# One more step ahead of six uses in the layer norm and feed-forward, and another way to lay out weights in the head, of a one-core scan kernel

## The chip, the cores and the metric

The kernel runs on one core of a Trainium2 chip. The metric is the device time of one launch in microseconds (us). The core has five engines with instruction streams of their own: TensorE (PE, with its weight loads shown as PEld), VectorE (DVE), ScalarE (ACT), GpSimd (POOL) and SyncE (SP), which here only issues DMAs.

## What is computed

The input is x, 4 images of 64x64 pixels with 96 channels. One launch runs a convolution and scan block, an attention block and a feed-forward block. The reference, cut to its main lines:

```python
def selective_scan(u, delta, A, Bs, Cs, D, delta_bias):
    delta = softplus(delta + delta_bias[None, :, :, None])
    def step(h, inp):
        ut, dt, Bt, Ct = inp
        dA = exp(dt[..., None] * A[None])
        h = dA * h + (dt * ut)[..., None] * Bt[:, :, None, :]
        return h, einsum('bkdn,bkn->bkd', h, Ct)
...
xp, z = split(bilinear(x, W_in, s_in, b_in), 2, axis=-1)      # sign weights, sign inputs
t = conv3x3(sign(xp + move0_b), Wb); t = prelu(t + conv_b + rp_b0) + rp_b1 + xp
xs = four directions of silu(t)                               # rows, columns, both reversed
dts, Bs, Cs = split(bilinear(xs, Wl, sl, bl)); dts = bilinear(dts, Wd, sd, bd)
A = -exp(A_logs)
y = sum of the four selective_scan outputs, each turned back to row order
y = (y - mean(y)) / sqrt(var(y) + 1e-5) * ln_w + ln_b
out = bilinear(y * silu(z), W_out, s_out, b_out)
```

192 channels with 16 states each are scanned over 4096 positions in 4 directions for each of the 4 images. The attention and feed-forward blocks that follow have layer norms of their own, over 96 channels.

## The kernel before, in words

**The order is written out by hand.** Instructions go to each engine's stream in the order in which the Python code issues them, and every engine is in order. Generators (`yield`) interleave the parts: a step is what a generator issues between two yields.

**The pieces.** `Scans.run` walks 1536 pieces, 384 an image, 96 a direction; the directions go in the order 1, 3, 0, 2. A piece is 32 of the channels with 4 of the states (128 partitions) by 1024 positions. For each piece ScalarE computes the decay `dA` (an Exp into PSUM, two buffers, L1531); GpSimd the injection `w` = dl times bc (L443, three pieces ahead); VectorE the scan (L443); VectorE or GpSimd the product with C (L443), chosen by `Tally`, which adds up estimated time for either; and TensorE the sum over states (L1604, four pieces later). L443 is the helper that counts, so many instructions share that line.

**The background.** After every piece `run` takes one step of one generator, `back`: the rest of image 0's prologue (projection, convolution, projections for the scan), the prologue of image 1, and then for each image: the turn of its fourth direction, the prologue of the image two further on, the layer norm and attention sums (`Epilogue.sums`, which calls `norm` for 8 blocks q of 512 columns, 11 steps each), the turn of the next image if its scans are far enough, and the feed-forward (`Epilogue.last`, 8 blocks of 12 steps). In `norm` and `last` a step typically writes a product into PSUM and the next step uses it: yc (L1131) by the square sq (L1191), the variance var by its logarithm (L1200), xc by xq (L1247), xv by `rstd` (L1136), kv (L1259) by kvs (L1264), and in `last` fv by `rstd`. The last image's norm and feed-forward run partly after the scans, in four lanes.

**The turn.** `turn` (L985 to L1013) loads the second column direction's output in 16 parts (yt, five of them ahead), copies each transposed into yh on ScalarE (L1003), and stores yh in two halves of 1.5 MB; yh has one buffer. `run` needs the turn of an image from its fourth direction on:

```python
            if i % NQ == 1:
                while KORD[self.pieces[i][1]] == 2 and self.pieces[i][0] not in c.turned:
                    next(back)
```

These lines (L1718) run the background on until the turn is done, ahead of piece i's other work.

**The head.** `weights` (from L160) loads and signs the weights while image 0's prologue starts; two steps of the prologue go to each one of `weights`. GpSimd's `omad` (L289) comes from the scales of the convolution (L276 to L289, reductions on VectorE); `transposed` (L193 to L201) puts transposes into one of two PSUM banks (y0, y1, shared with the prologue's projections ix and iz) and casts them out on VectorE. Delta's weights wd are transposed once (two calls), and 8 and 16 small stores (L331, L336) lay them on the diagonals of wdz and wdy. A's logs come in one load (al, L400), go through Exp on ScalarE (L402) and a sign change on VectorE (L403), and six DMAs (L405) lay them out as anm. The convolution's weighted row sums use a product with a ones matrix (tpw, L359). The prologue of image 0 runs 16 parts (2 halves by 8 blocks of 512 columns): ix and iz (L647, L648), tp (L653), the convolution cv (L745), v (L783), r (L784), the gate, u (L443), and copies for the next step.

**The DMA queue.** All loads and stores but a few small ones go through SP, in order; `Later` issues a store two steps after it was asked for (L462).

Of the kernel before, what the change touches and what calls it, by code (L numbers as in the profile page):

```python
# [53 lines left out]
def hybrid_kernel(ctx: ExitStack, tc: tile.TileContext, a: dict, out: bass.AP):  # L54
# [108 lines left out]
    def weights():  # L163
# [72 lines left out]
        nc.sync.dma_start(wo, a["w_out"])  # L236
        small = {}
# [18 lines left out]
        for t in gTs + [wdz, wdy]:  # L256
            nc.gpsimd.memset(t.bitcast(F32), 0.0)
# [16 lines left out]
        part = temp("part", [96, 2, 2])  # L274
        for i in range(2):
            for h in range(2):  # L276
                nc.vector.tensor_reduce(part[:, h, i : i + 1], cwn[h][i], AX.X, ALU.add, apply_absolute_value=True)
            yield
        nc.vector.tensor_tensor(csc, part[:, :, 0], part[:, :, 1], ALU.add)
        nc.vector.tensor_scalar(csc, csc, 1.0 / (9 * DN), None, ALU.mult)  # L280

        nc.vector.tensor_tensor(cbias, pv[:, :, CONV_B], pv[:, :, RP0], ALU.add)
        nc.vector.tensor_tensor(acs, pv[:, :, PRELU], csc, ALU.mult)
        nc.vector.tensor_tensor(acb, pv[:, :, PRELU], cbias, ALU.mult)
        nc.vector.tensor_tensor(acb, acb, pv[:, :, B_X], ALU.add)
        nc.vector.tensor_tensor(acb, acb, pv[:, :, RP1], ALU.add)
        nc.vector.tensor_scalar(oma, pv[:, :, PRELU], -1.0, 1.0, ALU.mult, ALU.add)
        for h in range(2):
            nc.gpsimd.tensor_scalar(omad[:, h], i96, oma[:, h : h + 1], None, ALU.mult)  # L289
        yield  # L290
# [5 lines left out]
        for o in range(2):  # L296
            m = negmean(f"wlm{o}", wl[o], DN)
            sw = temp(f"wls{o}", [128, DN], BF16)
            nc.scalar.activation(sw, wl[o], AF.Sign, bias=m)
            we = temp(f"wle{o}", [128, 4, 128], BF16)  # L300
            nc.gpsimd.memset(we, 0.0)
            for kk in range(2):
                rows = slice(64 * kk, 64 * kk + 64)
                for x, pair in enumerate(kinds[kk]):
                    for half, j in enumerate(pair):
                        if j is not None:
                            to, src = we[rows, x, 64 * half : 64 * half + 64], sw[rows, 64 * j : 64 * j + 64]
                            if o:
                                to = we[rows, x, half::2]
                            else:  # L310
                                to, src = to.rearrange("p (e i) -> p i e", e=2), src.rearrange("p (i e) -> p i e", e=2)
                            nc.gpsimd.tensor_copy(to, src)
            yield
            yield
            transposed(wR[:, o].rearrange("p x m -> p (x m)"), [we[:, x, :] for x in range(4)])
            yield


        wdt = []
        for x, t in enumerate(wd):  # L320
            wdm = negmean(f"wdm{x}", t, NR)
            wds = temp(f"wds{x}", [128, NK, NR], BF16)
            for k in range(NK):
                nc.scalar.activation(wds[:, k, :], t[:, k, :], AF.Sign, bias=wdm[:, k : k + 1])
            wdt.append(temp(f"wdt{x}", [NR, NK * 32]))
            yield
            transposed(wdt[x].bitcast(F8), [wds[:, k, :] for k in range(NK)])
            yield
        one, two = (t.rearrange("c (k d) -> c k d", k=NK) for t in wdt)
        for s in range(8):  # L330
            nc.sync.dma_start(wdz.bitcast(F32)[NR * s : NR * s + NR, :, s, :], one)  # L331
        yield
        for r0 in (0, 64):
            for s in range(8):
                at = r0 + NR * s
                nc.sync.dma_start(wdy.bitcast(F32)[at : at + NR, :, s, r0 // 4 : r0 // 4 + 16], two[:, :, 0:16])  # L336
        yield
# [12 lines left out]

        ones, diag = temp("ones", [96, 128]), temp("diag", [96, 4, 96])
        nc.vector.memset(ones, 1.0)
        for i in range(2):
            for h in range(2):
                col = pv[:, h, (LN_W, LN_B)[i] : (LN_W, LN_B)[i] + 1]
                nc.gpsimd.tensor_scalar(diag[:, 2 * i + h], i96, col, None, ALU.mult)
        yield
        ps = p.ps.tile([128, 512], F32, name="tpw", tag="y1")
        nc.tensor.matmul(ps[:, 0:384], ones, diag.rearrange("p i m -> p (i m)"), start=True, stop=True)  # L359
        for h in range(2):  # L360
            for o in range(2):
                nc.vector.tensor_tensor(
                    meanw[0:96, h, o], mean[:, int(h != o)], ps[0:96, 96 * o : 96 * o + 96], ALU.mult
                )
        nc.vector.tensor_copy(
            meanw[96:97, 0].rearrange("p o m -> p (o m)"), ps[96:97, 192:384]
        )
        yield
# [29 lines left out]
        yield  # L398
        al, al2 = temp("al", [128, 2, NK * NS]), temp("al2", [128, 2, 4, NK * NQ])
        nc.sync.dma_start(al, a["al"].rearrange("p h k s -> p h (k s)"))  # L400
        yield
        nc.scalar.activation(al, al, AF.Exp)  # L402
        nc.vector.tensor_scalar(al2, al.rearrange("p h (s j) -> p h j s", j=4), -1.0, None, ALU.mult)  # L403
        for g in range(NG):
            nc.sync.dma_start(anm[:, g, :], al2[32 * (g % 4) : 32 * (g % 4) + 32, g // 4])  # L405
# [133 lines left out]
def prologue(c, b, xts=None):  # L539
# [11 lines left out]
    with tc.tile_pool(name=f"xg_{b}", bufs=1) as xgp:  # L551
# [3 lines left out]
        with tc.tile_pool(name=f"cv_{b}", bufs=1) as cvp:  # L555
# [6 lines left out]
            def clear():  # L562
                nc.gpsimd.memset(xgw[64:128, 1], 0.0)
                for h in range(2):
                    nc.gpsimd.memset(tflat[h].bitcast(F32), 0.0)

            if alone:
                clear()

# [36 lines left out]
            def xfin(q, ps):  # L606
                n = CH if alone else 512
                cols = slice(n * q, n * q + n)
                nc.scalar.activation(xsT[:, cols], ps, AF.Sign, bias=negm, saturate=False)
                if alone:  # L610
                    t = c.p.w.tile([128, CH], F32, name=f"xb{q}_{b}", tag="w")[0:96]
                    nc.vector.tensor_scalar(t, ps, c.bo, None, ALU.add)
                else:
                    t = f32(f"xb{q}")[0:96]
# [3 lines left out]
            for q in range(4 if alone else NQ8):  # L618
                if alone:
                    ps = c.p.dA.tile([128, CH], F32, name=f"xps{q}_{b}", tag="dA")[0:96]  # L620
                    for i in range(8):
                        nc.tensor.transpose(ps[:, 128 * i : 128 * i + 128], xts[q][:, i, :], ident)
                else:
                    ps = bank(f"xps{q}", q % 2)[0:96]
                    for i in range(4):
                        nc.tensor.transpose(ps[:, 128 * i : 128 * i + 128], xts[q // 2][:, 4 * (q % 2) + i, :], ident)
                yield
                xfin(q, ps)
# [4 lines left out]
            if not alone:  # L633
                clear()
# [99 lines left out]
            def alone_parts():  # L734

                mid = end = None
                for n, part in enumerate(parts + [None, None]):
# [4 lines left out]
                    for s in range(4):  # L742
# [271 lines left out]
class Epilogue:  # L1014
# [143 lines left out]

    def norm(self, ln, q, got):
# [28 lines left out]
        yield  # L1188
        for h in range(2):
            t = f32(f"sq{h}")  # L1190
            nc.scalar.activation(t, sq[h], AF.Square)  # L1191
            sq[h] = t
# [5 lines left out]
        yield  # L1198
        sd, var, eps = (f32("sd"), ps[0:96], c.eps5[0:96]) if alone else (y0[96:97], ps[96:97], c.eps5[96:97])
# [45 lines left out]
        yield  # L1245
        t = f32("xq")
# [3 lines left out]
        yield  # L1250
        r = self.rstd(ln, f"xr{q}", ps)
# [8 lines left out]
        yield  # L1260
        kv = []
# [27 lines left out]
    def last(self, ln):  # L1289
# [25 lines left out]
        while nxt:  # L1315
# [28 lines left out]
            yield  # L1344
            r = self.rstd(ln, f"fr{q}", ps)
# [43 lines left out]
class Scans:  # L1389
# [250 lines left out]
    def start(self):  # L1640
# [35 lines left out]
        while lanes:  # L1676
            interleave(lanes)
        for n in range(3):
# [135 lines left out]
```

## Time and profile before

| | |
|---|---|
| median of 9 runs | 5379.89 us (5369.27 to 5382.63) |
| the profiled execution | 5372.74 us, of which the span is 5370.7 |
| granted TensorE clock, mean | 0.738 |
| first scan, last scan start | 184.26 us, 5248.73 us |
| busy: VectorE, GpSimd, ScalarE, TensorE | 93%, 92%, 67%, 63% |
| one scan (128x1024), one injection, one decay | 2.34, 2.36, 1.12 us |
| one product with C on VectorE, on GpSimd | 1.23, 2.36 us |

The profile shows one execution. Its page has the busy time of each engine, the span in 40 slices with the busy share of each in tenths, and groups of instructions of one line. A line of the waits reads: engine, the tile it was about to work on, what it waited for, then the total in us, how many times, and the longest. A line of the timeline reads: start, duration, engine, line, operation, tiles, count, and in brackets the idle time ahead of it with what ended it. In the windows view a line is one stretch: start and end, its length, then the busy time of PE, PEld, DVE, ACT and POOL with their instruction counts, the granted clock, the DMA share and GB/s.

### The profile page before, as it was taken

The numbers are of one execution on the slowest core, as the hardware profiler recorded it, in microseconds if no ns is written. First come the engines' busy times: TensorE is split into PE (matmuls) and PEld (weight loads), VectorE is DVE, ScalarE is ACT, GpSimd is POOL, SyncE is SP. The second block draws the span as 40 slices with busy tenths as digits, with TensorE's granted clock in tenths as the row PEclk, the third lists the DMA queues.
The fourth block names the chain that finished last, engine by engine and source line by source line (L and its number), as shares of the span: only waits on it lengthen the run. The fifth ranks groups of instructions, "written<-read, shape, count | busy, mean of one in ns | idle before, by whom it ended". The sixth has DMA issues, their size and how long they took to land. (4 is left out here: it accounts for less than half of the span.)

```text
span 5370.7 us, 61933 instructions
## 1 busy us (share of the span) xinstructions
PE 3377.4 (63%) x20029; PEld 1341.8 (25%) x20029; DVE 5005.1 (93%) x3163; ACT 3614.0 (67%) x5644; POOL 4954.6 (92%) x2255
## 2 busy tenths in 40 slices
PE   7357765467645776656775587566776664444577
PEld 3212222122222332212222233122232221111223
DVE  5699999999999999998999999999999999999995
ACT  6577767687766667777777666677656775565554
POOL 4699999999999999998999999999999999999990
PEclk8667877678866886777886678677787666666788
DMA  5666666867765666676765666766666565665652
GB/s 108 177 199 197 210 186 204 256 202 216 223 192 179 216 202 203 201 235 212 216 212 178 206 216 196 246 202 208 205 214 197 177 206 195 195 221 197 216 176 65
DMA packets 605500, 1068.83 MB, mean 199 GB/s; under 512 B 219740, under 2 KB 336885, under 8 KB 603381
## 3 DMA queue, kind: packets, MB, share of 16 engines
q1 hardware_dynamic: 602788, 1063.93, 64.1%
q8 instruction: 157, 2.57, 0.2%
q14 instruction: 171, 1.39, 0.1%
q0 software_dynamic: 1536, 0.79, 0.1%
q10 hardware_dynamic: 848, 0.15, 0.0%
HBM read 829.69 MB, written 228.30 MB: 197 GB/s over the span
## 5 line engine op out<-in xcount | busy, mean ns | idle before, releaser
L443 POOL TENSOR_TENSOR w<-dl,bc 128x1024 f32<-128x1024 f32 x1524 | 3551.1, 2357 | 54.4 <-PE yp L1604 31.3
L1531 ACT ACTIVATE dA<-dl,anm 128x1024 f32<-128x1024 f32 x1524 | 1701.2, 1116 | 488.9 <-DVE w L443 299.2
L443 DVE TENSOR_TENSOR_SCAN dA<-dA,cy,w 128x1024 f32<-128x1024 f32 x725 | 1698.5, 2343 | 75.9 <-ACT dA L1531 61.8
L443 POOL TENSOR_TENSOR w<-h,bc 128x1024 f32<-128x1024 f32 x570 | 1342.2, 2355 | 113.3 <-DVE h L443 106.9
L1604 PE MATMUL yp<-w,sum 128*32 128x256 f32 x12288 | 1246.6, 502 | 296.8 <-ACT pd L1485 208.8
L443 DVE TENSOR_TENSOR w<-dA,bc 128x1024 f32<-128x1024 f32 x966 | 1183.2, 1225 | 73.9 <-DMA bc<-bcd 11.0
L443 DVE TENSOR_TENSOR_SCAN h<-dA,cy,w 128x1024 f32<-128x1024 f32 x427 | 999.2, 2340 | 5.2 <-ACT dA L1531 4.6
L1604 PEld LDWEIGHTS yp<-w,sum 128*32 128x32 f32 x12288 | 317.0, 127 | 1352.7 <-issue 746.9
L1573 ACT COPY cy<-dA 128x1 f32<-128x1 f32 x725 | 113.9, 157 | 760.9 <-DVE w L443 758.3
L443 DVE TENSOR_TENSOR_SCAN dA<-dA,w 128x1024 f32<-128x1024 f32 x241 | 550.0, 2282 | 27.1 <-ACT dA L1531 24.2
L1466 PE MATMUL dps<-gT,wdz 128*128 128x64 fp8e5 x1008 | 114.5, 313 | 376.3 <-ACT ys L1618 374.4
L443 DVE TENSOR_TENSOR_SCAN h<-dA,w 128x1024 f32<-128x1024 f32 x143 | 325.9, 2279 | 22.4 <-POOL w L443 10.2
L1479 PE MATMUL dps<-sp,ident 128*128 128x512 f32 x378 | 263.4, 785 | 103.3 <-ACT dps L1475 103.2
L1609 PE MATMUL yp<-ya,back 128*128 128x256 f32 x576 | 219.9, 500 | 0.0
L1466 PEld LDWEIGHTS <-wdz 128*128 128x128 fp8e5 x1008 | 94.0, 152 | 452.0 <-issue 451.8
L1466 PE MATMUL dps<-gT,wdy 128*128 128x64 fp8e5 x504 | 57.6, 314 | 207.3 <-ACT ys L1618 207.2
L806 PE MATMUL cv<-tp,cwA 128*96 128x512 fp8e5 x432 | 150.9, 467 | 37.6 <-ACT r L838 36.5
L1573 ACT COPY cy<-h 128x1 f32<-128x1 f32 x427 | 79.2, 185 | 133.1 <-DVE h L443 132.4
L1131 PE MATMUL yc<-eys,mean 96*96 96x512 f32 x240 | 137.3, 726 | 48.2 <-DVE vks L443 24.4
L1471 ACT ACTIVATE pd<-dps,dbias,pvd 128x512 f32<-128x512 f32 x189 | 143.8, 761 | 9.0 <-PE dps L1466 8.9
L1472 ACT ACTIVATE sp<-dps,dbias,pvd 128x512 f32<-128x512 f32 x189 | 144.8, 766 | 0.0
L1609 PEld LDWEIGHTS yp<-ya,back 128*128 128x128 f32 x576 | 115.2, 231 | 117.3 <-issue 89.1
(379 smaller groups left out, 4488.1 us busy)
## 6 DMA issues: line engine op xcount, KB each, us to landing
dl<-dld SPq DMA_DIRECT2D x762, 512.0 KB
bc<-bcd SPq DMA_DIRECT2D x512, 512.0 KB
dld<-pd SPq DMA_DIRECT2D x126, 512.0 KB
yd<-ys SPq DMA_DIRECT2D x764, 64.0 KB
dld<-pd SPq DMA_DIRECT2D x126, 256.0 KB
ya<-yd SPq DMA_DIRECT2D x192, 128.0 KB
pu<-ud SPq DMA_DIRECT2D x32, 512.0 KB
pu<-utd SPq DMA_DIRECT2D x31, 512.0 KB
```

Source lines behind the costliest of these rows:

```text
L443: return getattr(self.eng, name)(out, *args, **kw)
L806: nc.tensor.matmul(ps, w[:, 96 * h : 96 * h + 96], tp[:, 8 * q + dy : 8 * q + dy + 8, dx : dx + IW], start=(w is taps[0][1]), stop=(w is t ...
L1131: self.c.nc.tensor.matmul(ps, w, x, start=(i == 0), stop=(i == len(pairs) - 1))
L1466: nc.tensor.matmul(pv[:, s], wd[:, k, s], gT[:, :, c0 : c0 + 16], start=(s == 0), stop=(s == 7))
L1471: nc.scalar.activation(d[:, 0], ps, AF.Abs, scale=sc, bias=bi)
L1472: nc.scalar.activation(t, ps, AF.Relu, scale=sc, bias=bi)
L1479: nc.tensor.matmul(ps, c.ident, t, start=False, stop=True, skip_group_check=True)
L1531: c.nc.scalar.activation(t, self.dlt[i // NQ][0], AF.Exp, scale=c.anm[:, g, NQ * KORD[e] + q : NQ * KORD[e] + q + 1])
L1573: self.c.nc.scalar.copy(self.carries[g, q], h[:, CH - 1 : CH])
L1604: c.nc.tensor.matmul(y[32 * x : 32 * x + 32, g % 2, :], c.sum4, prod[:, 256 * x : 256 * x + 256], start=(q == 0), stop=(q == NQ - 1 and no ...
L1609: c.nc.tensor.matmul(y[:, g % 2, :], w, src, start=False, stop=(n == len(more) - 1))
```

## The change

There are two parts. **In the epilogue** `room` adds one more yield, so one more piece, between six products and their first use, for images 0, 1 and 2: five in `norm` (ahead of sq, var's logarithm, xq, the rstd of xv, kvs) and one in `last` (the rstd of fv). **In the head** delta's signed weights are copied onto diagonals by GpSimd (40 small copies and three clears in e and wdf) and transposed in eight calls of `transposed`, eight transposes each, in place of two calls and 24 stores; the scales (and omad behind them) are computed after the first half of wR; the layer norm's weight rows come as six DMAs in place of the product with ones; A's logs come as 24 DMAs of single elements straight into anm, with Exp and sign change just before the first scan; GpSimd's clearing of xg and tp stands after the input's transposes in place of ahead of them; those are done in eight blocks of 512 columns in place of four of 1024; and u has a buffer per part and is stored in 16 parts in place of 8.

```diff
--- before.py
+++ after.py
@@ weights
+        wrow = temp("wrow", [96, 2, 96], F32)
+        for rows, h, s in halves(a["pv"][:, :, LN_W]):
+            nc.sync.dma_start(wrow[:, h, rows], s.partition_broadcast(96))
+        for rows, h, s in halves(a["pv"][:, :, LN_B]):
+            nc.sync.dma_start(meanw[96:97, 0, h, rows], s.unsqueeze(0))
...
-        for t in gTs + [wdz, wdy]:
+        for t in gTs + [wdz]:
             nc.gpsimd.memset(t.bitcast(F32), 0.0)
...
+        def scales():
+            part = temp("part", [96, 2, 2])
...
             for h in range(2):
-                nc.gpsimd.tensor_scalar(omad[:, h], i96, oma[:, h : h + 1], None, ALU.mult)
-        yield
+                nc.gpsimd.tensor_scalar(omad[:, h], i96, oma[:, h : h + 1], None, ALU.mult)
...
             transposed(wR[:, o].rearrange("p x m -> p (x m)"), [we[:, x, :] for x in range(4)])
             yield
+            if o == 0:
+                scales()
+                yield
...
-            wdt.append(temp(f"wdt{x}", [NR, NK * 32]))
-            yield
-            transposed(wdt[x].bitcast(F8), [wds[:, k, :] for k in range(NK)])
-            yield
-        one, two = (t.rearrange("c (k d) -> c k d", k=NK) for t in wdt)
         for s in range(8):
-            nc.sync.dma_start(wdz.bitcast(F32)[NR * s : NR * s + NR, :, s, :], one)
-        yield
-        for r0 in (0, 64):
-            for s in range(8):
-                at = r0 + NR * s
-                nc.sync.dma_start(wdy.bitcast(F32)[at : at + NR, :, s, r0 // 4 : r0 // 4 + 16], two[:, :, 0:16])
-        yield
+            nc.gpsimd.tensor_copy(e[:, :, s, NR * s : NR * s + NR], wds[0])
+        yield
+        for k in range(NK):
+            transposed(wdz[0:48, k].rearrange("p s d -> p (s d)"), [e[:, k, s, :] for s in range(8)])
+            yield
+        for k2 in range(0, NK, 2):
+            e = temp(f"wdf{k2}", [128, 2, 8, 128], BF16)
+            nc.gpsimd.memset(e, 0.0)
+            for r0 in (0, 64):
+                for s in range(8):
+                    at = r0 + NR * s
+                    nc.gpsimd.tensor_copy(e[r0 : r0 + 64, :, s, at : at + NR], wds[1][r0 : r0 + 64, k2 : k2 + 2])
+            yield
+            for k in range(2):
+                transposed(wdy[:, k2 + k].rearrange("p s d -> p (s d)"), [e[:, k, s, :] for s in range(8)])
+                yield
...
-                nc.gpsimd.tensor_scalar(diag[:, 2 * i + h], i96, col, None, ALU.mult)
-        yield
-        ps = p.ps.tile([128, 512], F32, name="tpw", tag="y1")
-        nc.tensor.matmul(ps[:, 0:384], ones, diag.rearrange("p i m -> p (i m)"), start=True, stop=True)
...
+                nc.vector.tensor_tensor(meanw[0:96, h, o], mean[:, int(h != o)], wrow[:, o], ALU.mult)
...
-        nc.sync.dma_start(al, a["al"].rearrange("p h k s -> p h (k s)"))
-        yield
-        nc.scalar.activation(al, al, AF.Exp)
-        nc.vector.tensor_scalar(al2, al.rearrange("p h (s j) -> p h j s", j=4), -1.0, None, ALU.mult)
         for g in range(NG):
-            nc.sync.dma_start(anm[:, g, :], al2[32 * (g % 4) : 32 * (g % 4) + 32, g // 4])
+            src = a["al"][32 * (g % 4) : 32 * (g % 4) + 32, g // 4].rearrange("d k (q j) -> j d (k q)", j=4)
+            for j in range(4):
+                nc.sync.dma_start(anm[j::4, g, :], src[j])
@@ prologue
-            if alone:
-                clear()
...
-                n = CH if alone else 512
-                cols = slice(n * q, n * q + n)
+                cols = slice(512 * q, 512 * q + 512)
...
             sub.close()
-            if not alone:
-                clear()
+            nc.gpsimd.memset(xgw[64:128, 1], 0.0)
+            for h in range(2):
+                nc.gpsimd.memset(tflat[h].bitcast(F32), 0.0)
...
-                            if eh == 0:
-                                us = c.p.h.tile([128, CH], F32, name=f"u{eq}_{b}", tag="h")[0:96]
-                            u = us[:, 512 * eh : 512 * eh + 512]
+                            u = f32("u" + en)[0:96]
                             c.vec.tensor_tensor(u, epz, e, ALU.mult)
-                            if eh:
-                                dst = c.ud[b].rearrange("h p l -> p h l")[:, :, 512 * eq : 512 * eq + 512]
-                                c.later.store(dst, us.rearrange("p (h l) -> p h l", h=2))
+                            c.later.store(c.ud[b][eh][:, 512 * eq : 512 * eq + 512], u)
@@ Epilogue
+    def room(self):
+
+        if self.b < NB - 1:
+            yield
+
...
                 sq.append(ps)
         yield
+        yield from self.room()
...
                 nc.vector.tensor_scalar(yc[h], yc[h], c.pv[:, h, LN_W : LN_W + 1], None, ALU.mult)
         yield
+        yield from self.room()
...
         mm(pc, [(c.mean96, x1)])
         yield
+        yield from self.room()
...
         mm(ps, [(c.on96, t)])
         yield
+        yield from self.room()
...
             nc.tensor.matmul(pk[i // 2][:, i % 2], tt[:, 128 * i : 128 * i + 128], c.wkv, start=True, stop=True)
         yield
+        yield from self.room()
...
             mm(ps, [(c.on96, t)])
             yield
+            yield from self.room()
             r = self.rstd(ln, f"fr{q}", ps)
@@ Scans.start
             interleave(lanes)
+        nc.scalar.activation(c.anm, c.anm, AF.Exp)
+        nc.vector.tensor_scalar(c.anm, c.anm, -1.0, None, ALU.mult)
```

More of the change, by code (lines that the diff above doesn't have):

```diff
@@ L272, in weights @@
         yield
-        part = temp("part", [96, 2, 2])
-        for i in range(2):
-            for h in range(2):
-                nc.vector.tensor_reduce(part[:, h, i : i + 1], cwn[h][i], AX.X, ALU.add, apply_absolute_value=True)
-            yield
[L279 to L289, printed above, removed]
-        yield
+        def scales():
+            part = temp("part", [96, 2, 2])
+            for i in range(2):
+                for h in range(2):
+                    nc.vector.tensor_reduce(part[:, h, i : i + 1], cwn[h][i], AX.X, ALU.add, apply_absolute_value=True)
+            nc.vector.tensor_tensor(csc, part[:, :, 0], part[:, :, 1], ALU.add)
+            nc.vector.tensor_scalar(csc, csc, 1.0 / (9 * DN), None, ALU.mult)
+            nc.vector.tensor_tensor(cbias, pv[:, :, CONV_B], pv[:, :, RP0], ALU.add)
+            nc.vector.tensor_tensor(acs, pv[:, :, PRELU], csc, ALU.mult)
+            nc.vector.tensor_tensor(acb, pv[:, :, PRELU], cbias, ALU.mult)
+            nc.vector.tensor_tensor(acb, acb, pv[:, :, B_X], ALU.add)
+            nc.vector.tensor_tensor(acb, acb, pv[:, :, RP1], ALU.add)
+            nc.vector.tensor_scalar(oma, pv[:, :, PRELU], -1.0, 1.0, ALU.mult, ALU.add)
+            for h in range(2):
+                nc.gpsimd.tensor_scalar(omad[:, h], i96, oma[:, h : h + 1], None, ALU.mult)
         kinds = (((0, 1), (2, None), (None, 0), (1, 2)), ((1, 0), (None, 2), (0, None), (2, 1)))
@@ L313, in weights @@
             yield
-            yield
             transposed(wR[:, o].rearrange("p x m -> p (x m)"), [we[:, x, :] for x in range(4)])
             yield
-        wdt = []
+            if o == 0:
+                scales()
+                yield
+        wds = []
         for x, t in enumerate(wd):
             wdm = negmean(f"wdm{x}", t, NR)
-            wds = temp(f"wds{x}", [128, NK, NR], BF16)
+            wds.append(temp(f"wds{x}", [128, NK, NR], BF16))
             for k in range(NK):
-                nc.scalar.activation(wds[:, k, :], t[:, k, :], AF.Sign, bias=wdm[:, k : k + 1])
-            wdt.append(temp(f"wdt{x}", [NR, NK * 32]))
-            yield
-            transposed(wdt[x].bitcast(F8), [wds[:, k, :] for k in range(NK)])
-            yield
-        one, two = (t.rearrange("c (k d) -> c k d", k=NK) for t in wdt)
-        for s in range(8):
-            nc.sync.dma_start(wdz.bitcast(F32)[NR * s : NR * s + NR, :, s, :], one)
-        yield
-        for r0 in (0, 64):
-            for s in range(8):
-                at = r0 + NR * s
-                nc.sync.dma_start(wdy.bitcast(F32)[at : at + NR, :, s, r0 // 4 : r0 // 4 + 16], two[:, :, 0:16])
-        yield
+                nc.scalar.activation(wds[x][:, k, :], t[:, k, :], AF.Sign, bias=wdm[:, k : k + 1])
+        e = temp("wde", [128, NK, 8, 48], BF16)
+        nc.gpsimd.memset(e, 0.0)
[4 more added lines that the diff above has]
+            transposed(wdz[0:48, k].rearrange("p s d -> p (s d)"), [e[:, k, s, :] for s in range(8)])
+            yield
+        for k2 in range(0, NK, 2):
+            e = temp(f"wdf{k2}", [128, 2, 8, 128], BF16)
+            nc.gpsimd.memset(e, 0.0)
+            for r0 in (0, 64):
+                for s in range(8):
+                    at = r0 + NR * s
+                    nc.gpsimd.tensor_copy(e[r0 : r0 + 64, :, s, at : at + NR], wds[1][r0 : r0 + 64, k2 : k2 + 2])
+            yield
+            for k in range(2):
+                transposed(wdy[:, k2 + k].rearrange("p s d -> p (s d)"), [e[:, k, s, :] for s in range(8)])
+                yield
         nc.vector.tensor_tensor(dbias, pvd[:, :, NK : 2 * NK], pvd[:, :, 2 * NK :], ALU.add)
@@ L349, in weights @@
         nc.vector.memset(mean[:, 1], -1.0 / DN)
[L351 to L355, printed above, removed]
-                nc.gpsimd.tensor_scalar(diag[:, 2 * i + h], i96, col, None, ALU.mult)
-        yield
-        ps = p.ps.tile([128, 512], F32, name="tpw", tag="y1")
-        nc.tensor.matmul(ps[:, 0:384], ones, diag.rearrange("p i m -> p (i m)"), start=True, stop=True)
         for h in range(2):
             for o in range(2):
[L362 to L367, printed above, removed]
-        yield
+                nc.vector.tensor_tensor(meanw[0:96, h, o], mean[:, int(h != o)], wrow[:, o], ALU.mult)
         nc.vector.tensor_copy(
@@ L397, in weights @@
             nc.sync.dma_start(sbR[r0 + 32 : r0 + 32 + NR, o, :], a["sl_dt"][k])
-        yield
-        al, al2 = temp("al", [128, 2, NK * NS]), temp("al2", [128, 2, 4, NK * NQ])
-        nc.sync.dma_start(al, a["al"].rearrange("p h k s -> p h (k s)"))
-        yield
-        nc.scalar.activation(al, al, AF.Exp)
-        nc.vector.tensor_scalar(al2, al.rearrange("p h (s j) -> p h j s", j=4), -1.0, None, ALU.mult)
         for g in range(NG):
-            nc.sync.dma_start(anm[:, g, :], al2[32 * (g % 4) : 32 * (g % 4) + 32, g // 4])
+            src = a["al"][32 * (g % 4) : 32 * (g % 4) + 32, g // 4].rearrange("d k (q j) -> j d (k q)", j=4)
+            for j in range(4):
+                nc.sync.dma_start(anm[j::4, g, :], src[j])
     c = SimpleNamespace(**locals())
@@ L560, in prologue @@
             sub = ExitStack()
[L562 to L565, printed above, removed]
-            if alone:
-                clear()
             if xts is None:
@@ L606, in xfin @@
             def xfin(q, ps):
-                n = CH if alone else 512
-                cols = slice(n * q, n * q + n)
+                cols = slice(512 * q, 512 * q + 512)
                 nc.scalar.activation(xsT[:, cols], ps, AF.Sign, bias=negm, saturate=False)
+                t = f32(f"xb{q}")[0:96]
                 if alone:
-                    t = c.p.w.tile([128, CH], F32, name=f"xb{q}_{b}", tag="w")[0:96]
                     nc.vector.tensor_scalar(t, ps, c.bo, None, ALU.add)
                 else:
-                    t = f32(f"xb{q}")[0:96]
                     nc.scalar.activation(t, ps, AF.Identity, bias=c.bo)
                 c.later.store(c.xbd[b][:, cols], t)
[L618 to L626, printed above, removed]
+            for q in range(NQ8):
+                ps = bank(f"xps{q}", q % 2)[0:96]
+                for i in range(4):
+                    nc.tensor.transpose(ps[:, 128 * i : 128 * i + 128], xts[q // 2][:, 4 * (q % 2) + i, :], ident)
                 yield
@@ L632, in prologue @@
             sub.close()
-            if not alone:
-                clear()
+            nc.gpsimd.memset(xgw[64:128, 1], 0.0)
+            for h in range(2):
+                nc.gpsimd.memset(tflat[h].bitcast(F32), 0.0)
             szs = {}
```

## The prediction

> **What bounds the kernel now.** I read the page's totals first.
>
> ```profile
> span 5370.7 us, 61933 instructions
> PE 3377.4 (63%) x20029; PEld 1341.8 (25%) x20029; DVE 5005.1 (93%) x3163; ACT 3614.0 (67%) x5644; POOL 4954.6 (92%) x2255
> DVE  5699999999999999998999999999999999999995
> POOL 4699999999999999998999999999999999999990
> ```
>
> VectorE and GpSimd share the work of the scan pieces (injection, scan, product) and are both full from the third slice to the last; ScalarE and TensorE have room. So a microsecond goes only if both of these two lose it: in the head (the first scan starts at 184.26), in idle time, or in work. Then I took busy time by stage: image 0's layer norm (89 pieces) and a stretch with no background work (67 pieces). The columns are the window, its length, then PE, PEld, DVE, ACT and POOL busy.
>
> ```profile
> 1712.70:2015.60 302.90, 236.09 (x1219) 90.10 (x1217) 291.30 (x193) 197.31 (x318) 293.19 (x128) 0.83 0.63 204
> 4461.50:4673.60 212.10, 87.37 (x637) 33.28 (x636) 209.13 (x120) 109.18 (x159) 208.00 (x90) 0.64 0.61 197
> ```
>
> A piece costs 302.90/89 = 3.404 us in the norm and 212.10/67 = 3.166 bare. VectorE idles 0.130 against 0.044 a piece, GpSimd 0.109 against 0.059. Third, the waits from 230 to 5280: what ScalarE waited for, and below it what VectorE and GpSimd did.
>
> ```profile
> ACT sq L1191 <- PE yc L1131: 64.8, 49, 2.9
> ACT xq L1247 <- PE xc L1131: 28.3, 24, 2.0
> ACT xr L1136 <- PE xv L1131: 25.0, 21, 2.7
> ACT kvs L1264 <- PE kv L1259: 24.6, 41, 1.2
> ACT eys L1200 <- PE var L1131: 19.6, 21, 1.8
> ACT fr L1136 <- PE fv L1131: 9.6, 10, 1.9
> ```
>
> ```profile
> DVE dA L443 <- ACT dA L1531: 86.0, 74, 2.2
> ```
>
> These are the six products of the change: a background step writes the product, one piece later ScalarE is already waiting for it, and the decay of the next piece stands behind that wait. They sum to 172 us, but VectorE waits only 86 us for decays in all: most of a 1 to 3 us wait is absorbed by the decay that is ready ahead.
>
> **The change part by part.**
>
> *1. One more step (room).* Ahead of five uses in the norm and one in the feed-forward, for images 0 to 2: 3x8x5 + 3x8x1 = 144 steps that issue nothing. A step with nothing in it costs a bare piece that would have come later anyway (stretches 1290-1357 and 1380-1470 have an idle lane), so 0 by itself. The gain is the idle time that goes. Excess idle of VectorE over bare: image 0 (0.130-0.044)x89 = 7.7; image 1 (0.137-0.044)x89 = 8.3; image 2 (0.188-0.044)x95 = 13.7: 29.6 us. Sorted by the 11 steps of a 512-column block, 0.98 us stands in the step ahead of sq and var and 0.26 in that of kv: about 1.1 above bare, x24 = 26. GpSimd's excess by the same sum: 4.5 + 5.5 + 11 = 21. Both must lose it, so 21 is the most likely ceiling; some products will still be late at one piece more, as the longest wait (2.9 us) is near a whole piece; so I take **-18**. Bounds: 0 (the idle moves to the next wait) and -44 (the norm's whole excess, 0.238x89 + 0.253x89 + 0.279x95 = 70, less its own vector work of 24x3.0 us spread over two engines = 36, is 34; and fv's 10).
>
> *2. What the longer norms push (forced turn).* The steps move the background by 40 pieces a norm and 8 a feed-forward. Image 2's turn (16 copies yh of 1.08 us each on ScalarE, with 16 loads and two 1.5 MB stores) stood at pieces 975-994; after norm 0, feed-forward 0 and norm 1 it is 80 to 88 later. Image 2's fourth direction begins at piece 1056, and L1718 then runs the background on until the turn is done: in the issue order of the changed program 13 of the 16 copies stand ahead of one decay (piece 1058). yh has one buffer, so half of them also wait for the first store to land. Price: 13x1.08 = 14; the store lands 7.7 to 11.6 us after its issue in the trace's three earlier turns, 9; the loads, only five of which are ahead, about 3: 26 us before a decay that takes 1.1. VectorE then holds two pieces, 2x3.25 = 6.5. Stall 26 + 1.1 - 6.5 = **+21**. Bounds: 14 + 1.1 - 6.5 = 9 (stores and loads hidden) and 14 + 12 + 12 + 1.1 - 6.5 = 33. Today's turn 2 costs nothing (3.141 us a piece, ScalarE idle 0.96 a piece), the cover that is lost. Image 1's turn now falls between norm 0 and feed-forward 0 and image 3's at 1407-1426 is 14 pieces before its need: neither is forced, 0.
>
> *3. The head.* Here I read the waits of 20 to 185 and the timeline. Scans start 49.4 us after xa, the last step of the convolution's prologue, and this part isn't touched; so the head's cost is the shift of the 16 convolution parts, whose v (L783) comes at 35.78, 40.85, 48.15, 57.58, 61.49, 71.23, 80.14, 92.85, 96.33 ... 127.25: 3.5 to 3.9 apart where nothing disturbs.
>
> ```profile
> POOL omad L289 <- DVE oma L287: 20.9, 1, 20.9
> ```
> ```profile
> 85.32 0.43 SPq L395 DMA_DIRECT2D sbR<-in_sl_bc  x1
> ...
> 92.32 0.31 ACT L402 ACTIVATE slab<-slab 128x128 f32<-128x128 f32 x1 [6.16 <-DMA slab<-in_al]
> ...
> 92.96 3.88 SPq L405 DMA_DIRECT2D anm<-slab  x6
> ...
> 96.47 0.59 PE L786 MATMUL cz<-xsT,winT 96*96 96x512 fp8e5 x1 [7.99 <-DVE u L443]
> ```
>
> (a) GpSimd is in order. The clearing of tp now stands behind omad, which waits for VectorE, and behind the second twelve weight copies (2.3 us), which wait for a sign on ScalarE at about 36; they end near 38.5, and the first tp can be written at about 40.4 in place of 24.46: +16. (b) Eight transposed calls of eight transposes, each with a VectorE cast of 48 or 128 x 1024 (about 1.3 us from the 0.68 of 512 columns), and GpSimd's memset and copies (4.2 us a half) take the place of two such calls. They share the y banks with the first parts; today's four such stalls of TensorE are 2.1 to 3.1 us each. At 1.4 a call: +11, so part 3 comes at 57.58 + 27 = 84.5. (c) Parts 4 to 15 then need 12x3.7 = 44. Today parts 4 to 9 lose 23 above that pace: 8 to the wait for al (6.16 on ScalarE, 7.99 on TensorE), which goes; about 7 to the wd and tpw work, whose 24 small stores keep SP (wdz 6.39 us, wdy 12.72) and which go; 8 stay. (d) SP gets 24 loads of A's logs of single elements after the 12 of sbR; at 3.88/6 = 0.65 us each 15.5 us, with sbR some 20, ahead of the u store of part 3, whose buffer part 9 or 10 needs: +4.5. Part 15: 84.5 + 44 + 8 + 4.5 = 141 against 127.25: **+14**. Bounds: +2 (nothing stays: 129) and +27 (nothing is given back). The Exp and sign change of A before the first scan (0.6 us) lie beside the 45.8 us in which the first injection waits for its deltas; xfin in eights and u by 512 columns: 0, beside the wait in (a).
>
> The 24 new loads are the place where a rule speaks against the change. The Trainium skill ("DMA: Bandwidth & Descriptors", Rules for kernel authors) says that a strided last dimension turns into one descriptor per element, and its Bandwidth section gives about 10.5 ns a packet as the floor of small ones. As an estimate from that page, 24x512 elements over 16 engines are 768 packets each, 8 us; by it (d) would be SP's issue time still, since 8 is under 15.5. The nearest row is the 16 stores wdy of 12.72 us, and (d) is taken from the rows.
>
> *Sum.* +14 - 18 + 21 = +17. The profiled run took 5372.74 (span 5370.7 and 2.0 around it), the median is 5379.89. On the profiled run that is 5389.7; on the median, which I predict, **5396.9**, +0.3%.
>
> **The rivals.** About 0.2%, 10.8 us (5369.1 and 5390.7), is what a measurement of this kernel can tell.
>
> *A. The head runs free (faster).* All 36 us that the 16 parts lose today above 3.7 a part come from what is removed. Then tp starts 16 late, but part 15 comes at 35.8 + 16 + 15x3.9 = 110: -17. Sum -17 - 18 + 21 = -14: 5366. For it: the largest stall is al's. Against: 16 late leaves GpSimd's copies and eight transposes on the same engines at the same time. It decides once the head is worth -14 or better.
>
> *B. Covered or cheap (no change).* The burst of copies falls where ScalarE is ahead, or its loads and store are ready: 9 in place of 21, +5, 5385; or the head is worth +2: also +5. For it: ScalarE is idle a third of the time. Against: the wait for the yh store can't be hidden by idle time.
>
> *C. Room does nothing.* The waits move to the next use, or the products are late because TensorE runs the pieces' sums first (0.83 clock in the norm): +14 + 0 + 21 = +35, 5415. For it: TensorE is busier here (236 of 303 us) than anywhere. Against: the waits are mostly under one piece.
>
> **How the numbers follow.** Forecast 0.52 (its own range 5391 to 5412), A 0.12, B 0.22, C 0.14. Faster 0.12, same 0.22, slower 0.52 + 0.14 = 0.66. Range 5368 to 5420: down to A's price, up past C's, leaving out about 0.07 below and 0.08 above.
>
> **What would show it.** First scan near 198. The six waits of ScalarE, 172 us, under 60, and norms at about 3.30 us a piece over 129 pieces. At pieces 1056-1058, ahead of image 2's fourth direction, a row of yh copies and a gap on VectorE of about 21 us. If the first scan comes before 186, (a) or (b) is wrong; if the norm's pace stays, room; if no gap stands there, the turn.

## The result and the profile after

The changed kernel takes 5398.5 us (median of 10 runs, 5391.35 to 5403.52) against 5379.63 (30 runs): ratio 1.0035, 95% interval 1.0027 to 1.0043. The forecast was 5396.9. The profiled execution took 5400.29 (span 5398.5). As the kernel before was profiled in a run 7 us below its median, the two profiles differ by 27.8 us and the medians by 18.9; from here on times are compared by medians and ratios, and profiles only stage by stage.

The page of the changed kernel, with the lines that answer to those shown of before:

```profile
span 5398.5 us, 62109 instructions
...
PE 3403.4 (63%) x20083; PEld 1357.3 (25%) x20083; DVE 5011.1 (93%) x3171; ACT 3609.3 (67%) x5648; POOL 4960.2 (92%) x2293
...
DVE  4599999999999999999999999998999999999995
POOL 3599999999999999999999999998999999999990
```

The first slices are emptier: the head is longer. The first scan starts at 211.67 (184.26 before), the last 5064.8 us after it (5064.5 before). So the profiles put the whole difference into the head, and all else comes out at zero. It isn't made of zeros. The six waits of ScalarE from 230 to 5300 (the line numbers are those of the changed kernel):

```profile
ACT sq L1171 <- PE yc L1105: 13.2, 12, 2.4
...
ACT xq L1229 <- PE xc L1105: 6.5, 5, 1.6
...
ACT xr L1110 <- PE xv L1105: 4.9, 5, 1.4
ACT kvs L1248 <- PE kv L1242: 4.4, 7, 1.2
...
ACT eys L1181 <- PE var L1105: 2.7, 3, 1.6
```

The rstd of fv doesn't wait any more; 32 us are left of 172. Image 0's norm, in the windows view, now runs 126 pieces in 410.1 us, 3.255 a piece against 3.404:

```profile
1740.90:2151.00 410.10, 283.96 (x1557) 113.56 (x1559) 405.34 (x258) 252.65 (x391) 408.12 (x177) 0.78 0.63 203
```

Yet VectorE's waits for decays grew, and the longest is 24.2 us (last column). The timeline of the changed kernel shows where, at the start of image 2's fourth direction:

```profile
DVE dA L435 <- ACT dA L1516: 106.0, 70, 24.2
```
```profile
3689.82 4.08 ACT L977 COPY yh<-yt 96x512 f32<-96x512 f32 x4
...
3699.50 2.03 ACT L977 COPY yh<-yt 96x512 f32<-96x512 f32 x2 [5.61 <-DMA yt<-yd]
3701.56 0.30 SPq L984 DMA_DIRECT2D y<-yh  x1
...
3710.32 7.72 ACT L977 COPY yh<-yt 96x512 f32<-96x512 f32 x8 [8.79 <-DMA y<-yh]
...
3717.98 1.13 ACT L1516 ACTIVATE dA<-dl,anm 128x1024 f32<-128x1024 f32 x1
...
3719.21 2.30 DVE L435 TENSOR_TENSOR_SCAN dA<-dA,w 128x1024 f32<-128x1024 f32 x1 [24.19 <-ACT dA L1516]
```

Fourteen copies in a row (13.8 us), 5.6 for a load, 8.8 for the store of yh, then the decay, and VectorE's scan after 24.2 us of idling. This is the forced turn as it was forecast (13 copies, 3 and 9). VectorE's waits for bc, before and after:

```profile
DVE w L443 <- DMA bc<-bcd: 11.0, 6, 6.7
```
```profile
DVE w L435 <- DMA bc<-bcd: 1.9, 2, 1.2
```

The head of the changed kernel, on ScalarE, GpSimd, SP and VectorE:

```profile
40.80 0.78 ACT L631 ACTIVATE tp<-ix,sbx,pvx 128x512 fp8e5<-128x512 f32 x1 [4.42 <-POOL tp L612]
```
```profile
34.28 1.03 POOL L294 TENSOR_SCALAR omad<-ident,oma 96x96 f32<-96x96 f32 x2 [7.84 <-DVE oma L292]
...
36.52 2.32 POOL L316 COPY slab<-slab 64x64 bf16<-64x64 bf16 x12 [0.74 <-ACT slab L303]
...
39.76 1.96 POOL L612 MEMSET tp<- 128x1089 f32 x2
```
```profile
109.42 16.95 SPq L397 DMA_DIRECT2D anm<-in_al  x24
126.47 1.52 SPq L454 DMA_DIRECT2D ud<-u  x3
128.09 0.62 SPq L454 DMA_DIRECT2D utd<-ut  x1
128.80 5.16 SPq L454 DMA_DIRECT2D ud<-u  x1
134.04 0.60 SPq L454 DMA_DIRECT2D utd<-ut  x1
134.74 5.29 SPq L454 DMA_DIRECT2D ud<-u  x1
```
```profile
129.53 0.81 DVE L757 TENSOR_SCALAR v<-cv,acs,acb 96x512 f32<-96x512 f32 x1 [8.96 <-DMA ud<-u]
...
136.61 0.69 DVE L435 TENSOR_TENSOR u<-cz,e 96x512 f32<-96x512 f32 x1 [4.53 <-DMA ud<-u]
```

The first tp waits for GpSimd's clearing, which stands behind omad and the weight copies, and comes at 40.80 (forecast 40.4). Part 3's v comes at 82.97 (84.5), part 9's at 116.13, 13 us later than before. Then the 24 loads hold SP for 17 us, the u stores stand behind them, and part 15 comes at 155.39, 28 later than before.

### The profile page after: what moved, and what is told of

Its sections match the earlier page's. It is cut to its first block, busy times and chain, and to the rows that moved or that the text cites. A ratio compares the mean times of both kernels' runs of the same rounds, so it can differ in the third digit from the quotient of the medians.

```text
span 5398.5 us, 62109 instructions
## 1 busy us (share of the span) xinstructions
PE 3403.4 (63%) x20083; PEld 1357.3 (25%) x20083; DVE 5011.1 (93%) x3171; ACT 3609.3 (67%) x5648; POOL 4960.2 (92%) x2293
## 5 line engine op out<-in xcount | busy, mean ns | idle before, releaser
L1242 PE MATMUL kv<-wkv,tt 97*128 97x192 f32 x240 | 78.9, 501 | 135.2 <-DVE tt L435 135.1
```

The lines of the kernel that those rows point to most:

```text
L1242: nc.tensor.matmul(pk[i // 2][:, i % 2], tt[:, 128 * i : 128 * i + 128], c.wkv, start=True, stop=True)
```

## The experiments

Theory after the result: the head costs some 27 us, the steps gain some 24, the forced turn costs as much. Its rivals: that steps and turn are both worth nothing; that the head is worth the forecast's 14. The kernel before ran again beside each group of kernels (medians 5379.3 to 5381.5), and each ratio is to those runs; the last two columns are from one profile of each kernel.

| kernel | median us | ratio to before, 95% interval | first scan at | first to last scan |
|---|---|---|---|---|
| before | 5379.6 | | 184.3 | 5064.5 |
| changed | 5398.5 | 1.0035 (1.0027 to 1.0043) | 211.7 | 5064.8 |
| head_only | 5410.1 | 1.0054 (1.0040 to 1.0068) | 215.4 | 5072.2 |
| room_only | 5365.9 | 0.9974 (0.9963 to 0.9985) | 184.3 | 5055.6 |
| room_free | 5350.5 | 0.9946 (0.9934 to 0.9959) | 183.4 | 5044.8 |
| late_turn | 5394.1 | 1.0027 (1.0017 to 1.0038) | 183.1 | 5087.2 |
| moves_only | 5367.1 | 0.9975 (0.9966 to 0.9984) | 183.9 | 5055.9 |
| anm_early | 5381.8 | 1.0006 (0.9997 to 1.0015) | 200.9 | 5055.4 |
| pool_free | 5389.9 | 1.0018 (1.0009 to 1.0027) | 208.4 | 5050.7 |
| diag_old | 5379.6 | 1.0004 (0.9995 to 1.0012) | 197.8 | 5060.8 |
| head_two | 5382.7 | 1.0003 (0.9994 to 1.0012) | 200.5 | 5058.2 |
| head_three | 5379.6 | 0.9998 (0.9989 to 1.0007) | 194.4 | 5056.6 |
| phase_swap | 5368.4 | 0.9978 (0.9969 to 0.9987) | 183.7 | 5058.6 |
| best | 5342.1 | 0.9926 (0.9913 to 0.9938) | 185.0 | 5030.8 |

**head_only.** The changed kernel with all six lines `yield from self.room()` taken out.

> The changed head with the six extra steps taken out again. Theory (head costs about 27 us, the extra steps gain about 24 and the forced turn of image 2 costs about 24): first scan at 211 to 212 us, the stretch from first to last scan 5064 us as in the kernel before, time +19 to +28 us over the kernel before (medians 5399 to 5408). Rival (the steps and the turn are both worth about nothing): the same +19 to +28, so this run only sizes the head. Rival (the head is worth what was forecast, +14, and the steps lose the rest): first scan near 198, +14.

+29 us, a little over what was expected, first scan 215.4: the head by itself costs more than the whole change. The changed kernel has the same head and had its first scan at 211.7, so that two profiles of this head differ by 3.8 us. Behind the head, head_only's code is that of before, but its scans take 5072.2 us where before's profiled run took 5064.5: nearly 8 us of scatter between two profiles of the same code, most of it in image 2's norm (3.513 a piece against 3.445).

**room_only.** The other half: before with `room` and its six calls.

> The kernel before with the six extra steps alone, head as before. Theory: first scan at 184; 14 copies of image 2's turn ahead of one decay, a gap of 24 us on VectorE there, and the rest of the scans 24 us shorter: 0, within 5 us of the kernel before. Rival (the steps lose on their own, as forecast with less gain): +3 to +12.

0.9974, -14 us, nearly three times the 5 that the theory allowed. The gap is there with 24.2 us and 8.8 for the store, so the steps gain more than the turn costs.

**room_free.** As room_only, with image 2's turn ahead of its need (image 2's scans of the column direction are done in the middle of image 1's norm):

```diff
@@ sums, after each block's norm
+            n = self.b + 1
+            if ln is self.lane and n < NB and n not in c.turned and self.scans.done(n, 2):
+                yield from turn(c, n)
```

> The kernel before with the six extra steps, and image 2's turn run between two blocks of image 1's norm, 80 pieces earlier, so that nothing is forced at image 2's fourth direction. Theory: no gap over 5 us on VectorE at pieces 1054 to 1062, -20 to -24 us (5356 to 5360). Rival (both steps and turn are worth nothing): 0. Rival (the turn in the norm delays the norm's products again): -10.

-29 by the ratio, more than the 20 to 24 expected. The wait of 24.2 is gone; the longest wait for a decay is 3.7:

```profile
DVE dA L443 <- ACT dA L1545: 82.4, 70, 3.7
```

The forced turn is worth 0.9974 - 0.9946 = 0.0028, 15 us of time, not its gap of 24.

**late_turn.** Before, with the forced turn alone.

```diff
+                    for _ in range(81 if b == 1 else 0):
+                        yield
                     yield from turn(c, b + 1)
```

> The kernel before without any of the extra steps ahead of products, but with 81 empty steps ahead of image 2's turn, so that 14 of its 16 copies are issued ahead of one decay as in the changed kernel. Theory: +20 to +26 us, a gap on VectorE of about 24 us at the start of image 2's fourth direction. Rival (the burst is covered, or made up for later): under +8.

Between the two: the gap is 24.1 us, the time +14.5 by the ratio. Two runs agree that some 9 us of the gap are not in the time. A candidate is that the delay moves image 2's norm, too; the next run bears on it.

**moves_only.** Before without any step ahead of a product, with the stages moved by empty steps.

```diff
+            for _ in range(40 if b == 2 else 0):
+                yield
             yield from e.sums(e.lane)
...
-                if scans.done(b + 1, 2, 20):
+                if scans.done(b + 1, 2, 45):
```

> The kernel before without any step ahead of the products: image 1's turn right behind image 0's norm, as in the changed kernel, and empty steps so that image 2's norm starts at piece 1168, not 1097. Nothing is forced. Theory (of the 30 us that the six steps gained with no forced turn, 18 are the products and 12 come from where the stages now stand, which the steps moved): -10 to -13 us. Rival (the products are all of the 30): 0, within 3 us.

-13 by the ratio: the theory holds, and the rival falls. Where it comes from is in the trace of before, eight pieces from the start of image 1's fourth direction (672): 32.6 us there, 25.2 in moves_only. Of before, SP and VectorE:

```profile
2406.10 0.32 SPq L1010 DMA_DIRECT2D y<-yh  x1
2407.50 9.84 SPq L430 DMA_DIRECT2D xt<-in_x  x4
2417.38 1.98 SPq L1508 DMA_DIRECT2D dl<-dld  x2
2419.45 0.55 SPq L1497 DMA_DIRECT2D bc<-bcd  x1
```
```profile
2427.10 1.23 DVE L443 TENSOR_TENSOR w<-dA,bc 128x1024 f32<-128x1024 f32 x1 [6.66 <-DMA bc<-bcd]
```

Image 1's turn ended just as its fourth direction began; image 3's four input loads follow the turn, hold SP for 9.8 us, and the scan's own bc load comes behind them. With the turn 60 pieces earlier this is gone (in the changed kernel VectorE waits 1.9 us for bc in all, before 11.0). The rest of the 13 us lies in image 2's norm, which starts later, and is not taken apart further.

**anm_early.** The changed kernel, the loop with `nc.sync.dma_start(anm[j::4, g, :], src[j])` moved from behind sbR to ahead of the first of the eight calls.

> The changed kernel with its 24 element-wise loads of A's logs issued some 50 us earlier, where SP stands idle ahead of the first gate store (46 to 69 us), in place of behind sbR. Theory (the head's miss is term (d): the 24 loads hold SP for 17 us ahead of the u stores and cost 15 us, not 4.5): first scan at 196 to 198 in place of 211.7, part 10's v without a wait for a u store, time +4 over the kernel before in place of +19. Rival (part 10's wait comes from the element-wise landings of ut and from 16 u stores, which stay): first scan above 206.

First scan at 200.9, 10.8 us earlier, part 10 at 122.5 in place of 129.5; the time falls by 17. The loads cost as much issue time where nobody waits:

```profile
45.75 17.52 SPq L339 DMA_DIRECT2D anm<-in_al  x24
```

So the place of these loads, (d), is most of what the head's term missed. In the first scan it is 11, not the 15 that I expected; in the time it is 16 to 17.

**pool_free.** The changed kernel with `clear()` and the scales where before has them.

> The changed kernel with GpSimd's clearing of xg and tp and the convolution's scales back at their places in the kernel before. Theory (the first tp waits for the clearing, then the eight input transposes set it): first tp at 31 to 33 in place of 40.8, first scan 6 to 9 us earlier (203 to 206), time +10 to +13 over the kernel before. Rival (the parts' start is paid back before part 9 in any case): first scan within 2 us of 211.7. Rival (term (a) is all 16): first scan near 196.

The first tp comes at 34.5, later than the 31 to 33 expected, and the first v 6.4 us earlier. The first scan is at 208.4, 3.2 us earlier, between the theory (6 to 9) and the rival (within 2); the time is 9 us less by the ratio, as the theory had it. The 3.2 can't be read alone: half of the early start is gone by part 3 (79.56 against 82.97), before SP's 24 loads begin, and against head_only's profile, where the clearing is late too, every part from 3 to 15 and the first scan come 6.7 to 7.4 us earlier.

**diag_old.** The changed kernel with the two calls and 24 small stores of before for wdz and wdy.

> The changed kernel with delta's weights laid on their diagonals by two transposed calls and 24 small stores, as in the kernel before; all else of the changed head stays. Theory (the eight calls cost 9 us up to part 3, and by part 9 the stores' queue has taken as much): part 3's v 9 us earlier than 83, first scan within 4 us of 211.7. Rival (term (b) stays to the end): first scan near 201, time +8 over the kernel before.

The theory fell, the rival holds: part 3 10.6 us earlier, about as expected, and the first scan 13.9 earlier (197.8); the time is +2, where the rival had +8. What the trace points to is the issue order: with fewer steps in `weights` the 24 loads start at 79 in place of 109, when fewer u stores stand behind them.

**head_two.** Both undone, the loads ahead of the 24 stores.

> The changed kernel with both undone: delta's weights laid on their diagonals by 24 small stores as before, and the 24 loads of A's logs issued ahead of these in SP's idle time. Theory (the two costs are apart: the calls hold parts 0 to 3 back by 10.6 us, the loads hold the u stores back behind part 9 by 11): first scan 25 us earlier than in the changed kernel, 187, time -8 under the kernel before. Rival (one wait hides behind the other, since the parts end on SP's queue in any case): first scan near 197, as with either alone, time as the kernel before.

First scan 200.5: the rival. The two gains don't add; SP is then busy from 45 to 81 with 48 small transfers and the first u store waits (VectorE 8.4 us). So each of the two edits, with the other in place, only moves work within one queue.

**head_three.** head_two with pool_free's edit.

> The changed kernel with three things undone: delta's diagonals by small stores, the loads of A's logs in SP's idle time, and GpSimd's clearing with the convolution's scales at their places of before. With the first two alone the first scan is at 200.5, as with either alone. Theory (what is left of the head's cost is the late first tp, once nothing on SP holds the parts back behind it): first tp 34.5 in place of 40.8 and the first scan 6 us earlier, 194; time -6 under the run with two undone, 5377. Rival (the parts still end on SP's stores of u): first scan 199 to 201.

194.4, as the theory has it: the first tp is 6.6 us earlier than in head_two and the first scan 6.0. The time falls by 3, not by the 6 expected. The 10 us to 184.3 that remain are with what still differs (eight input transposes in place of four, six loads of weight rows, 16 u stores in place of 8); in this trace the first tp is already 9.7 us later than before (34.17 against 24.46). Which of the three does it was not tried.

**phase_swap.** room_only, with image 0's and image 1's norm begun 3 pieces later (the added lines hold a norm's first block until the piece number fits).

```diff
+                if self.todo == START and (self.scans.at - {0: 5, 1: 4}.get(self.b, self.scans.at)) % 8:
+                    yield
+                    continue
```

> The kernel before with the six extra steps, image 0's norm begun 3 pieces later and image 1's 3 later: a block now takes 16 pieces, so all blocks of a norm begin at the same piece of the scan's groups of eight (0, 7, 2 for the three images with the steps alone; here 3, 2, 2). In the run with no forced turn image 2's norm stood at 3 and cost 3.346 us a piece, here at 2 3.255. Theory (the place in the eight sets the pace): image 0's norm 3.254 to about 3.34 a piece, image 1's from 3.302 down to about 3.26; time within 6 of the run of the steps alone (the forced turn has two copies more). Rival (the pace is the image's, or chance): 3.254 and 3.302 stay within 0.02.

Half right. Over 124 pieces from the first sq (by the starts of the scans in the trace), image 0 goes from 3.260 to 3.295 and image 1 from 3.315 to 3.265 a piece, so the place in the groups of eight counts (the rival asked for no change over 0.02); but image 0 loses 4 us, not 10. Each is read from one profile; image 1's 3.265 lies below all its values at 7 (3.299 to 3.361 over eight kernels).

**best.** room_free without the step ahead of fv, with norms placed by phase_swap's lines (images 1 and 2 at 4) and two empty steps behind the turn in the norm.

> The head of the kernel before, five of the six steps (not the one of the feed-forward), image 2's turn between two blocks of image 1's norm with two empty steps behind it, and norms begun so that all blocks stand at 0 or 2 of the eight. Theory (place in the eight counts): image 2's norm 3.255 a piece in place of 3.346, 8 to 15 us under the run with no forced turn, 5336 to 5343. Rival (it doesn't): 5350, or 5352 without the feed-forward's step.

5342.1, ratio 0.9926 to before: 8 us under room_free, at the weak end of what was expected. Image 2's norm takes 3.272 a piece where room_free's took 3.356, and the longest wait for a decay is 2.2 us:

```profile
DVE dA L443 <- ACT dA L1552: 73.6, 64, 2.2
```

This version beats both kernels, by 0.74% and, by the ratios, 1.1%. Besides image 2's norm it moves image 1's to place 2 and leaves out the step ahead of fv, so the 8 us are not image 2's norm alone.

## Why the forecast came out right

It was right in sign and within 2 us, but by terms that cancel: that it came so near is luck. Against the steps as they stand on record:

- *Room, -18.* Right in size. The whole gain with no forced turn is 29 to 30 (room_free), the moves alone give 12 to 13 (moves_only), so 16 to 18 is left for the products. That is a difference between two kernels whose image 2 norms stand at different places; the products with nothing moved were not run. (By the row shown, GpSimd's idle time in the bare stretch is 4.10/67 = 0.061 a piece, not 0.059; the ceiling of 21 stays.)
- *"Neither is forced, 0" of the moved stages.* Wrong. The moves were priced only for harm. Image 1's turn in its old place cost time that the waits of before show (11.0 us for bc, 6.7 the longest), and I read that line without asking whether the change would move its cause. -13 us were missing from the sum.
- *The forced turn, +21.* The mechanism is the forecast's step by step, the gap 24.2. In the time it is worth 15. Where the other 9 go stays open: in late_turn image 2's norm moves as well, and in room_free that norm stands in a worse place of the eight (3.356 against 3.253); so neither pair is clean. The traces show where it comes back, counted from the first scan: late_turn is 22.6 us behind head_only, whose scans run the code of before, at piece 1088, 6.4 at 1216 and 15.0 at the last; room_free is 20.5 ahead of room_only at 1088, 6.3 at 1280 and 10.8 at the last. Both times that is the stretch in which image 2's norm runs.
- *The head, +14.* Too small by half: +29 by head_only, +27 by the profile, and the first scan at 211.7 where 198 was the sign. (a), tp at 40.4, came at 40.80, by the wait it named; but with the clearing and the scales back (pool_free) tp comes at 34.5, not at 24.5, and the input's last xsT ends at 32.9 there where before had 24.6: the later input, which the prediction put at 0 beside that wait, stands right behind it. (b), part 3 at 84.5, came at 82.97. Up to part 9 the shift fell to 13, as (c) had it. The step that failed is the size of (d), the +4.5. The issue time was right (15.5 forecast, 16.95 measured); what was left out is who stands behind it: three u stores, then the utd stores in pieces of 64 bytes, after each of which the next u store holds SP for 5 us or more. The last six parts took 39 us where 6x3.7 = 22 were counted. As diag_old and head_two show, the head's terms aren't additive at all; what they share is SP's queue, in which the u stores stand.
- By rows of this case the sum would have been +29 - 17 - 13 + 15 = +14; measured is +19, which the scatter of the runs allows. One place where the 5 may lie is image 1's norm: with the same code it runs at 3.360 a piece in the changed kernel's profile and at 3.315 in room_only's, 5.6 us over 124 pieces. Rival C (the steps do nothing) is refuted by the waits and moves_only with room_free, rival A (the head runs free) by the first scan, rival B's covered turn by the gap.
- The Trainium skill ("DMA: Bandwidth & Descriptors", Rules for kernel authors) says that a strided last dimension becomes one descriptor per element. The trace agrees: anm_early has 12,769 packets under 512 bytes between 45.7 and 70 us, and 24 loads of 512 elements make 12,288. What held the rest up was the loads' issue time, 0.71 us each and 17 in all; the estimate of 8 us of packets, worked out from that page, is under it.

## What to carry to other kernels

Price a moved stage for what its old place cost, not only for what its new place may cost: read each wait of the profile near the old place, and ask what is queued ahead of it. For a batch of small transfers count all that stands behind it in the queue until the queue is level again, not only the first. And where several edits feed one in-order queue, run them together as well as apart, since their prices don't add.

## What was not expected of the hardware and the schedule

- On SP a store of 6,144 pieces of 64 bytes (utd) takes 0.6 us to issue, and the next store or load then takes 5.0 to 5.3, once 6.5 (in the changed kernel): the price shows on the one behind.
- A load of 512 single elements takes 0.71 us of issue (16.95 for 24), and six short loads of weight rows 7.4 and 4.8 us for three each.
- With 16 steps a block, each block of a norm stands at the same place of the scan's groups of eight pieces, and its pace goes with it: at 0 3.260 us a piece in all nine profiles with the steps and a norm at 0, at 2 3.253 to 3.272, at 3 3.295 and 3.356, at 7 3.30 to 3.36. Why 7 ranges so far, in kernels of which most differ only in the head, is open.
